# The attention's output projection, moved from the tail into the last chunk of the attention

## The chip, the cores and the metric

The kernel runs on one core of one Trainium2 chip. The metric is the device time of one launch in microseconds (us). Before the change the median of three runs is 10759.1 us (10754.76 to 10764.04). About 0.2% can be told from no change.

## What is computed

A four-layer graph network on N = 3327 nodes with 128 features and a dense 0/1 adjacency matrix. Only layer 1, an attention, and the start of layer 2 matter here.

```
def _L1_gnn_ref(x, spatial_encoding, edge_encoding, Wq, Wk, Wv, Wo):
    n, d = x.shape
    h = Wq.shape[0] // d
    scale = d ** (-0.5)
    q = (x @ Wq.T).reshape(d, n, h)
    k = (x @ Wk.T).reshape(d, n, h)
    v = (x @ Wv.T).reshape(d, n, h)
    a = jnp.einsum('dnh,dmh->dnm', q, k) * scale
    a = a + spatial_encoding + edge_encoding
    a = jax.nn.softmax(a, axis=2)
    out = jnp.einsum('dnm,dmh->dnh', a, v)
    out = out.reshape(n, h * d)
    return out @ Wo.T
...
    # --- layer 1 (adj_preln) ---
    h = jnp.maximum(_layernorm(x, axis=-1), 0.0)
    x = x + _L1_gnn_ref(h, adj, adj, L1_gnn_Wq, L1_gnn_Wk, L1_gnn_Wv, L1_gnn_Wo)
    # --- layer 2 (adj_preln) ---
    h = jnp.maximum(_layernorm(x, axis=-1), 0.0)
    x = x + _L2_gnn_ref(h, adj, ...)
```

There are 128 heads (d) of 8 features (h). The reshape is a plain one: the result in the order head, node, feature is cut into 3327 rows of 1024. So row r of what meets Wo holds the 128 pairs of head and node from 128 r on, and four heads in a row fill 4 x 3327 / 128, about 104 rows. A row is complete once the heads that it holds are done for all of its nodes.

## The kernel before, in words

**Order.** Layer 0, then the projections to queries, keys and values (written to device memory as qf, kf, vd), then the attention, then `tail`, which holds the output projection and layers 2 and 3. All but the tail stand in a manual schedule: each engine executes its instructions in the order in which the program emits them. In the tail the framework orders the instructions by itself, and what depends on nothing in the attention may be put far ahead (the load and scaling of the degrees, L1202 to L1204, runs in the attention's last chunk).

**The attention.** The queries are cut into seven chunks of 476 columns (the last has 471, handled as 472). In each chunk the 128 heads go by in 32 groups of four. In a group, the 26 tiles of 128 keys are worked off in blocks: in the first chunk pairs, later eight blocks of three tiles and one of two. For a block of three tiles:

- PE makes the scores of 12 (tile, head) pairs, in products of one to three heads (L926). Nine go to DVE, which adds the doubled adjacency tile and writes `p_early` (L942; sums of two heads or one, 944 or 472 elements). Three go to `late`.
- ACT takes the exponential of `late` (L956, 1416 elements) and of `p_early` (L947, 4248 elements).
- POOL multiplies the late ones by exp of the adjacency (L958).
- PE weighs: it multiplies by the values, with a column of ones for the sums of the softmax, into `acc` (L969). It weighs about eight tiles behind the products.

Within a block the order is a string, such as "aWAWbWBlc" and, every other block, "cWaWAbWlB"; the block of two has "WcWalA" or "WaWAlc". Letters a, A, b, B and c are products and sums, W weighs a tile, l is the late part. The score banks are two pairs in PSUM, taken in turn (`banks.pair()`), so PE runs at most two products ahead of DVE's sums. `late` has one buffer, p_early four.

**Between blocks** `events(c, g, t, ...)` is called for each tile t of the block just emitted. At t = 4 it loads the next group's keys (SP). At t = 8 it loads the next group's queries and values: a POOL memset of one column (L649), eight query loads (L654) and four value loads (L639), all issued by SP. When the last tile of a group has been weighed, in the third block of the next group, DVE copies `acc` out (L980) and SP stores it to `ot` in device memory with four DMAs (L985). `ot` has nine rows, eight features and the sum.

**The tail** first loads x (`xs_late`, L1092), which waits for the last store of the 16-bit adjacency (L887), and then projects: for 26 tiles of rows, a load of `o` from `ot` (L1185), the reciprocal of the sums (L1187, DVE), the division (L1188, DVE), eight transposes (L1193, PE), two copies of the transposed tile (L1194, ACT), eight products with Wo (L1197, PE, two instructions each), and the addition to x (L1198, DVE). `done` starts a piece of the layernorm (L162 to L169) and the split into two 16-bit parts (L219, L223) whenever its tiles are there: pieces of 4, 9 and 13 tiles. Then comes layer 2's aggregation over the adjacency, 14 products per tile (L235), and, after each second tile, four transposes of h (L1223).

Of the kernel before, what the change touches and what calls it, by code (L numbers as in the profile page):

```python
# [20 lines left out]
P = 128  # L21
N = 3327
# [34 lines left out]
def kernel(  # L57
# [83 lines left out]
    def in_pieces(f, cuts=CUTS):  # L141

        todo = [slice(t0, t1) for t0, t1 in zip(cuts, cuts[1:]) if t1 > t0]

        def done(t):
            while todo and todo[0].stop <= t:
                p = todo.pop(0)
                f(p, p.stop - p.start)

        return done  # L150

    def layernorm_relu(pool, then=None, tmp=None):

        h = pool.tile([P, T, D], F32, name="h")
        xc = (tmp or pool).tile([P, T, D], F32, name="ln_xc")
        sq = (tmp or pool).tile([P, T, D], F32, name="ln_sq")
        mean = pool.tile([P, T], F32, name="ln_mean")
        var = pool.tile([P, T], F32, name="ln_var")
        rstd = pool.tile([P, T], F32, name="ln_rstd")

        def piece(p, n):
            nc.vector.tensor_reduce(mean[:, p], xs[:, p], AX.X, ALU.add)  # L162
            nc.vector.tensor_scalar_mul(mean[:, p], mean[:, p], 1.0 / D)
            nc.vector.tensor_sub(xc[:, p], xs[:, p], over_t(mean, p.start, n))
            nc.scalar.activation(sq[:, p], xc[:, p], AF.Square)
            nc.vector.tensor_reduce(var[:, p], sq[:, p], AX.X, ALU.add)
            nc.scalar.activation(rstd[:, p], var[:, p], AF.Sqrt, bias=eps_c, scale=1.0 / D)
            nc.vector.reciprocal(rstd[:, p], rstd[:, p])
            nc.vector.scalar_tensor_tensor(h[:, p], xc[:, p], 0.0, over_t(rstd, p.start, n), op0=ALU.max, op1=ALU.mult)  # L169
            if then is not None:  # L170
                then(h, p, n)

        return h, in_pieces(piece)

    def load_rows(dst, src, t, col0, w):

# [92 lines left out]
    vd = dpool.tile([GP, EA], F32, name="vd")  # L269
    ot = dpool.tile([EA, GP], F32, name="ot")  # L270
    adj16 = dpool.tile([T, P, N], BF16, name="adj16")
    keyd = dpool.tile([NH // 4, P, NP], F16, name="keyd")

    q_chunks = chunks(N, QW)
# [241 lines left out]
    for n, t in enumerate(order):  # L516
        kp = rows_of(t)
        if t in kept:
            part_products(acc, n, parts1, t, kept[t], range(len(CS)), False)
            src = kept[t][:kp, : q_chunks[0][1]]  # L520
        else:
            a = early_a.pop(0) if early_a else load_a(t)
            part_products(acc, n, parts1, t, words(a)[:, :, 1], range(len(CS)), False)
            src = a[:kp, : q_chunks[0][1]]
        firsts[t] = doubled(adj_pools[0], src, t, q_chunks[0][1])
        add_to_sum(firsts[t], 0, n == 0)
        if n == 0:
            nc.vector.tensor_reduce(x_max, x1.rearrange("p t d -> p (t d)"), AX.X, ALU.max, apply_absolute_value=True)
        if n == 1:
            bit_limits()  # L530
            nc.gpsimd.dma_start(vd[N * NH : N * NH + 1, :], zero[:1, :EA])
            for end in (qf, kf):
                nc.gpsimd.dma_start(end[:E, N * NH :], zero[:E])
    for t in TAIL:
# [41 lines left out]
    class Parting:  # L576
# [7 lines left out]

        def load(self, side):
            src = SIDES[side][0]
            self.raw[side] = kq0.tile([E * JW, WJ], F32, name="raw")
            nc.sync.dma_start(self.raw[side], self.rows(src, 0))

        def part(self, side, i):  # L590
            if i == 0:
                self.hi[side] = kq0.tile([E * JW, WJ], F16, name="hi")
                self.lo[side] = kq0.tile([E * JW, WJ], F16, name="lo")
            p = slice(i * W4, min((i + 1) * W4, WJ))
            raw, hi = self.raw[side][:, p], self.hi[side][:, p]
            nc.gpsimd.tensor_copy(hi, raw)
            nc.gpsimd.tensor_sub(self.lo[side][:, p], raw, hi)  # L597
# [6 lines left out]
        def at(self, t):  # L604

            for side, t0 in ((0, 6), (1, 16)):
                if t0 <= t < t0 + 4:
                    self.part(side, t - t0)
                if t == t0 + 4:
                    self.store(side)  # L610
            if t == 10:
                self.load(1)

    PARTING_TILES = (6, 7, 8, 9, 16, 17, 18, 19)

# [176 lines left out]
    for r in range(T):  # L792
# [27 lines left out]
                early.pop(0)()  # L820
        if r % 2 and r // 2 < len(CS):
            store_x(r // 2)
        if r == 1:
            dp = ps.tile([P, 512], F32, name="tp")
            end = sum_columns(0, dp)
            sums = l1.tile([P, 512], F32, name="deg_sums", bufs=1)
            for n, c0, c1 in ((SUM_ROWS, QW, end - 1), (QW % SUM_ROWS, end - 1, end)):
                nc.vector.tensor_copy(sums[:n, c0:c1], dp[:n, c0:c1])
            store_sums(0, sums)
            nc.sync.dma_start(degd[:, N:], zero[:1, :1])  # L830
# [41 lines left out]
    with tc.tile_pool(name="at_in", bufs=1) as a_pool, tc.tile_pool(name="at_p", bufs=4) as p_pool, tc.tile_pool(  # L872
# [114 lines left out]
        with tc.manual_schedule(engines=engines), ExitStack() as ctx_ps:  # L987
# [19 lines left out]
                n_weighed += 1  # L1007

            def events(c, g, t, n, a_in):
                nonlocal coming, part, ahead_part, n_stored, k_next  # L1010
                more = n < len(groups)
                if t == 8 and more:
                    coming = first[n] if n < len(first) else load_rest(*groups[n])
# [19 lines left out]
                if t == 6 and c + 1 < len(q_chunks):  # L1033
                    for _ in range(min(len(to_store), 1 + T // n_groups)):
                        store_adj(*to_store.pop(0))
                    a_in += [load_adj(c + 1, i) for i in range(len(a_next), T * (g + 1) // n_groups)]
                if t == T - 4 and c + 1 < len(q_chunks):
                    for a, i, w in a_in:
                        a_next.append(doubled(adj_pools[(c + 1) % 2], a[: rows_of(i), :w], i, w))
                        to_sum.append((a_next[-1], c + 1, i == 0))  # L1040
                        to_store.append((c + 1, i, a_next[-1]))

            coming = part = None
            for n, (c, g) in enumerate(groups, 1):
                if n > 1:
                    q4, v4 = coming
# [8 lines left out]
                for i, size in enumerate(TRIPLES if c else PAIRS):  # L1055
# [9 lines left out]
                    for step in order:  # L1065
                        if step == "W":
                            if n_tiles + heads / 2 >= n_weighed + ahead:
                                weigh_next()
                        elif step == "l":
                            block.late_ones()  # L1070
                        else:
                            pos, which = PIECES[step] if step != "c" else (size - 1, (3,))
                            heads += len(which)
                            block.sums(pos, which, c > 0)
                    n_tiles += size
                    n_block += 1
                    for t in range(t0, t0 + size):
# [4 lines left out]
                            e_next.append(exp_of(a_next[late_tiles[len(e_next)]], c + 1))  # L1082
            while to_weigh:
                weigh_next()
            for a in to_store:
                store_adj(*a)

# [67 lines left out]
    def tail(general):  # L1155
# [13 lines left out]
        with ExitStack() as s:  # L1169
# [3 lines left out]
            def halved(h, p, n):  # L1173
                split_unless_general(parts, h, p, scale=PART)

            h, done = layernorm_relu(pool, halved)
            with tc.tile_pool(name="lo", bufs=3) as lo, tc.tile_pool(name="lo_ps", bufs=2, space=PSUM) as ps:
                wo_s = lo.tile([NH, E, D], F32, name="wo_s", bufs=1)
                nc.gpsimd.dma_start(wo_s, wo)
                for t in range(T):  # L1180
                    kp = rows_of(t)
                    o = lo.tile([P, EA, NH], F32, name="o")
                    src = ot.rearrange("e (p t c) -> t p e c", t=T, c=NH)[t]
                    for p0, p1 in ((0, kp),) if kp == P else ((0, 112), (112, kp)):
                        nc.sync.dma_start(o[p0:p1], src[p0:p1])  # L1185
                    inv = lo.tile([P, NH], F32, name="inv")
                    nc.vector.reciprocal(inv[:kp], o[:kp, E, :])  # L1187
                    nc.vector.tensor_mul(o[:kp, :E, :], o[:kp, :E, :], inv[:kp].unsqueeze(1).to_broadcast([kp, E, NH]))  # L1188
                    oT = lo.tile([NH, E, P], F32, name="oT")
                    for quad in range(2):  # L1190
                        tp = ps.tile([P, 4, P], F32, name="tp")
                        for j in range(4):
                            nc.tensor.transpose(tp[:, j, :kp], o[:kp, 4 * quad + j, :], ident[:kp, :kp])  # L1193
                        nc.scalar.copy(oT[:, 4 * quad : 4 * quad + 4, :kp], tp[:, :, :kp])  # L1194
                    yp = ps.tile([P, D], F32, name="yp")
                    for e in range(E):
                        nc.tensor.matmul(yp[:kp], oT[:, e, :kp], wo_s[:, e, :], start=(e == 0), stop=(e == E - 1))  # L1197
                    nc.vector.tensor_add(xs[:kp, t, :], xs[:kp, t, :], yp[:kp])  # L1198
                    done(t + 1)

            if not general:
                nc.sync.dma_start(deg, degd.rearrange("o (p t) -> (o p) t", t=T))  # L1202
# [404 lines left out]
```

## Time and profile before

| what | us |
|---|---|
| median of three runs | 10759.1 |
| the profiled execution's own time | 10759.11 |
| its span, first to last instruction | 10757.4 |
| DVE, ACT, PE, POOL busy in the span | 10089.7, 9935.9, 9785.6, 7294.7 |
| L942 DVE, sums of the scores | 9151.8 |
| L947 and L956 ACT, exponentials | 8123.9 and 3908.6 |
| L958 POOL, products of the late part | 6397.6 |
| last L969 ends, first L235 starts | 10036.35, 10145.50 |

Busy times are of the hardware profiler; an instruction can start in its engine's pipeline before the one ahead of it has left, so the sum over a line can exceed its share of the span. A wait is written as idle time before an instruction, with what ended it. The profile also gives the TensorE clock that was granted, as a share of full speed: 0.988 on average.

### The profile page before, as it was taken

What the parts mean: (1) busy time and instruction counts of PE and PEld (TensorE: products, weight loads), DVE (VectorE), ACT (ScalarE), POOL (GpSimd) and SP (SyncE); (2) the same over time, 40 slices, a digit from 0 to 9 for tenths busy, and PEclk for the clock granted to TensorE, in tenths of its full rate; (3) what the DMA queues carried; (4) which work ended last, traced back from release to release, by engine and by line L of the source; (5) the groups of instructions that cost most, each with busy time, mean ns of one, the idle gap of its engine ahead of it and who ended that gap; (6) DMA issues with size and microseconds to landing.
All of it is one profiled execution on the core that took longest, in us unless ns stands there. A gap on an engine that the chain in (4) does not pass through costs nothing. (4 is left out here: it accounts for less than half of the span.)

```text
span 10757.4 us, 183790 instructions
## 1 busy us (share of the span) xinstructions
PE 9785.6 (91%) x74235; PEld 2140.8 (20%) x74268; DVE 10089.7 (94%) x11602; ACT 9935.9 (92%) x4716; POOL 7294.7 (68%) x3314
## 2 busy tenths in 40 slices
PE   7899999999989999899999999999999989999897
PEld 3211111111111111111111111111111111111453
DVE  5799999999999999999999999999999999999666
ACT  2799999999999999999999999999999999999432
POOL 3388887777777777777777777777777766666203
PEclk9999999999999999999999999999999999999998
DMA  8644433111111111111111111111111111111422
GB/s 294 205 105 104 103 99 87 45 42 45 45 42 45 44 44 43 45 45 43 46 44 44 42 45 46 42 45 43 43 42 44 46 36 38 35 37 38 160 92 101
DMA packets 462641, 709.21 MB, mean 66 GB/s; under 512 B 56587, under 2 KB 391419, under 8 KB 456150
## 3 DMA queue, kind: packets, MB, share of 16 engines
q1 hardware_dynamic: 458596, 690.86, 21.7%
q8 instruction: 585, 9.58, 0.4%
q0 software_dynamic: 3184, 6.51, 0.2%
q14 instruction: 276, 2.26, 0.1%
HBM read 557.43 MB, written 139.73 MB: 65 GB/s over the span
## 5 line engine op out<-in xcount | busy, mean ns | idle before, releaser
L942 DVE TENSOR_TENSOR p_early<-early,a 128x952 f32<-128x952 f32 (+3 forms) x10336 | 9151.8, 957 | 172.3 <-PE early L926 141.3
L947 ACT ACTIVATE p_early<-p_early 128x4284 f32<-128x4284 f32 (+3 forms) x2144 | 8123.9, 3789 | 8.9 <-DVE p_early L942 8.5
L958 POOL TENSOR_TENSOR p_late<-p_late,e 128x1428 f32<-128x1428 f32 (+3 forms) x2144 | 6397.6, 2984 | 2521.4 <-ACT p_late L956 2505.8
L969 PE MATMUL acc<-p_early,v 128*9 128x476 f32 (+3 forms) x33728 | 5704.9, 565 | 126.7 <-issue 114.4
L956 ACT ACTIVATE p_late<-late 128x1428 f32<-128x1428 f32 (+1 forms) x2144 | 3908.6, 1823 | 12.4 <-DMA vd<-v_st 5.3
L926 PE MATMUL early<-q,k_in 32*128 32x476 f16 (+1 forms) x14784 | 3058.5, 366 | 440.1 <-DVE p_early L942 417.3
L969 PE MATMUL acc<-p_late,v 128*9 128x476 f32 (+3 forms) x12864 | 2101.0, 565 | 0.2 <-POOL p_late L958 0.2
L926 PEld LDWEIGHTS <-k_in 32*128 32x128 f16 x19968 | 764.9, 91 | 5446.0 <-issue 5425.1
L926 PE MATMUL late<-q,k_in 32*128 32x476 f16 (+1 forms) x5184 | 778.5, 367 | 178.8 <-ACT p_late L956 178.6
L969 PEld LDWEIGHTS acc<-p_early,v 128*9 128x9 f32 (+1 forms) x33728 | 655.6, 88 | 1197.1 <-issue 1038.7
L926 PE MATMUL early<-q,k 32*128 32x476 f16 x2080 | 395.6, 368 | 6.9 <-DVE p_early L942 5.2
L969 PEld LDWEIGHTS acc<-p_late,v 128*9 128x9 f32 (+1 forms) x12864 | 240.5, 88 | 458.4 <-issue 363.0
L235 PE MATMUL agg_ps<-a,part 128*128 128x512 bf16 (+1 forms) x1067 | 240.8, 378 | 53.1 <-issue 47.4
L926 PEld LDWEIGHTS <-k 32*128 32x128 f16 x3328 | 121.3, 91 | 786.5 <-issue 770.5
L194 ACT ACTIVATE agg<-agg_ps 128x512 f32<-128x512 f32 x9 | 4.7, 598 | 256.6 <-PE agg_ps L235 256.6
L358 PE MATMUL agg_ps<-a,part 128*128 128x512 bf16 (+4 forms) x720 | 171.1, 395 | 56.6 <-DMA a<-in_adjT_dram 55.3
L666 DVE TENSOR_REDUCE k<-k_in 128x256 f16<-128x256 f16 x377 | 221.8, 588 | 0.0
L285 POOL TENSOR_SCALAR a<-a_in 128x476 bf16<-128x476 f32 (+2 forms) x156 | 219.0, 1404 | 0.5
L597 POOL TENSOR_TENSOR lo<-raw,hi 96x278 f16<-96x278 f32 (+1 forms) x256 | 182.3, 712 | 20.5
L296 POOL TENSOR_TENSOR deg_half<-deg_half,a 128x476 f32<-128x476 f32 (+1 forms) x175 | 191.9, 1096 | 2.1
L955 PE MATMUL late<-a,two_i 128*128 128x476 bf16 x544 | 182.2, 373 | 0.0
L1386 PE MATMUL sp<-yT,hT 128*128 128x512 f32 (+1 forms) x364 | 171.3, 612 | 11.6 <-ACT agg L1391 5.7
(289 smaller groups left out, 2693.2 us busy)
## 6 DMA issues: line engine op xcount, KB each, us to landing
k_in<-keyd SPq DMA_DIRECT2D x192, 832.0 KB
v<-vd SPq DMA_DIRECT2D x896, 117.0 KB
a<-in_adjT_dram SPq DMA_DIRECT2D x39, 1663.5 KB
a<-adj SPq DMA_DIRECT2D x78, 831.8 KB
a_in<-in_adjT_dram SPq DMA_DIRECT2D x125, 238.0 KB
keyd<-k SPq DMA_DIRECT2D x416, 64.0 KB
k_in<-kt SPq DMA_DIRECT2D x240, 104.0 KB
q<-qt SPq DMA_DIRECT2D x1520, 14.9 KB
```

Source lines behind the costliest of these rows:

```text
L235: nc.tensor.matmul(acc[c][:, :w], part[:, t, :], a[:, c0 : c0 + w], start=(t == 0 and i == 0), stop=(t == T - 1 and i == len(parts) - 1),)
L285: nc.gpsimd.tensor_scalar(a2[:kp, :w], a, 2.0 * S_SCALE, None, op0=ALU.mult)
L296: nc.gpsimd.tensor_tensor(deg_half[:, :w], deg_half[:, :w], a2[:, :w], op=ALU.add)
L597: nc.gpsimd.tensor_sub(self.lo[side][:, p], raw, hi)
L666: nc.vector.tensor_reduce(k, src.unsqueeze(3), AX.X, ALU.max)
L926: return nc.tensor.matmul(sp[:, : self.we], self.keys(self.t0 + pos)[r], self.q4[r, : self.we], start=True, stop=stop)
L942: Block.first_sum = nc.vector.tensor_tensor(p, scores, a2, op=ALU.add)
L947: nc.scalar.activation(p, p, AF.Exp, scale=1.0 / S_SCALE)
L955: nc.tensor.matmul(late[:, i, :we], two_i, self.a[pos][:, :we], start=False, stop=True)
L956: nc.scalar.activation(self.late[:, :, :we], late[:, :, :we], AF.Exp, scale=1.0 / S_SCALE)
L958: nc.gpsimd.tensor_tensor(g, g, self.e[:, :we].unsqueeze(1).to_broadcast([P, self.n_g, we]), op=ALU.mult)
L969: nc.tensor.matmul(acc[32 * i : 32 * i + EA, :w], self.v4[:kp, i, t, :], p[:kp, :w], start=(t == 0), stop=(t == T - 1),)
```

## The change

Four edits belong together.

1. A class `Rows` works off the rows of one head group: `load` fetches them from `ot` (about 104 rows of 9 x 128, two DMAs), `invert` and `divide` make the softmax's division, `turn` transposes the eight features, and `project` multiplies by Wo and stores about 104 rows of the product to a new scratch `yo` (two DMAs).
2. In the last chunk, group g does this for group g - 1: load at event t = 11, reciprocal on DVE at t = 14, division on POOL in two halves at t = 17 and t = 20, the transposes in the eighth block behind its step "A", with the copy on DVE, and the projection in the ninth block behind its step "A". Both take a pair of score banks. Wo is loaded by SP in the first group, into the buffers that the first chunk's key pairs used. The last group's rows follow after the last weighing, with the division on DVE, and ahead of the last store of the adjacency.
3. The tail loads `yo` in three DMAs (the last five partitions hold what the last group wrote), adds it to x in five pieces of 2, 4, 6, 7 and 7 tiles, and starts the layernorm in the same pieces. The old projection stays for a general case that isn't run here.
4. To make room, the buffers `raw`, `hi` and `lo` of the first chunk get a shape that `Rows` can share, hi and lo as halves of one tile. The degree sums of the first chunk move from row tile 1 to row tile 12 of the layer's projections. A row of zeros is written to the end of `yo`.

```
+    yo = dpool.tile([NP, D], F32, name="yo")
...
+            nc.gpsimd.dma_start(yo[N:], zero[:1, :D])
...
-            self.raw[side] = kq0.tile([E * JW, WJ], F32, name="raw")
+            self.raw[side] = kq0.tile([P, EA * NH], F32, name="raw")[: E * JW, :WJ]
...
-                self.hi[side] = kq0.tile([E * JW, WJ], F16, name="hi")
-                self.lo[side] = kq0.tile([E * JW, WJ], F16, name="lo")
+                parts = kq0.tile([P, 2, WJ + 1], F16, name="parts")
+                self.hi[side], self.lo[side] = (parts[: E * JW, j, :WJ] for j in range(2))
...
+    class Rows:
+        def __init__(self, g):
+            self.r0 = 4 * g * N // NH
+            self.m = 4 * (g + 1) * N // NH - self.r0
+            self.pieces = ((0, 96), (96, self.m))
+        def load(self):
+            self.o = kq0.tile([P, EA * NH], F32, name="raw").rearrange("r (e c) -> r e c", c=NH)
...
+            for p0, p1 in self.pieces:
+                nc.sync.dma_start(self.o[p0:p1], src[self.r0 + p0 : self.r0 + p1])
+        def invert(self):
+            nc.vector.reciprocal(self.inv, self.o[: self.m, E, :])
+        def divide(self, engine, e0, n):
+            o = self.o[: self.m, e0 : e0 + n]
+            engine.tensor_tensor(o, o, self.inv.unsqueeze(1).to_broadcast([self.m, n, NH]), op=ALU.mult)
+        def turn(self, tp):
+            m = self.m
+            for e in range(E):
+                nc.tensor.transpose(tp[:, e // 4, e % 4 * m : (e % 4 + 1) * m], self.o[:m, e, :], ident[:m, :m])
+            nc.vector.tensor_copy(self.oT.rearrange("c (a r) -> c a r", a=2), tp[:, :, : 4 * m])
+        def project(self, yp, wo_s):
+            m = self.m
+            for e in range(E):
+                nc.tensor.matmul(yp[:m, 0, :D], self.oT[:, e * m : (e + 1) * m], wo_s[e], start=(e == 0), stop=(e == E - 1))
+            nc.vector.tensor_copy(self.y, yp[:m, 0, :D])
+            for p0, p1 in self.pieces:
+                nc.sync.dma_start(yo[self.r0 + p0 : self.r0 + p1], self.y[p0:p1])
...
-        if r == 1:
+        if r == 12:
...
+                if c + 1 == len(q_chunks) and g == 0 and t == 2:
+                    for e in range(E):
+                        k = kq0.tile([P, 2, P], F16, name="k", bufs=KEYS_AHEAD + 1)
+                        wo_s.append(k.bitcast(F32).rearrange("p a b -> p (a b)"))
+                        nc.sync.dma_start(wo_s[e], wo[:, e, :])
+                if c + 1 == len(q_chunks) and g:
+                    if t == 11:
+                        rows = Rows(g - 1)
+                        rows.load()
+                    if t == 14:
+                        rows.invert()
+                    if t in (17, 20):
+                        rows.divide(nc.gpsimd, 0 if t == 17 else 4, 4)
...
+                        if step == "A" and rows and i == 7:
+                            rows.turn(banks.pair()[0])
+                        if step == "A" and rows and i == 8:
+                            rows.project(banks.pair()[0], wo_s)
+                            rows = None
...
+            rows = Rows(n_groups - 1)
+            rows.load()
+            rows.invert()
+            rows.divide(nc.vector, 0, E)
+            rows.turn(banks.pair()[0])
+            rows.project(banks.pair()[0], wo_s)
             for a in to_store:
                 store_adj(*a)
...
+            h, done = layernorm_relu(pool, halved, cuts=CUTS if general else X_CUTS)
+            if not general:
+                y = pool.tile([P, T, D], F32, name="y")
+                by_slot = yo.rearrange("(p t) d -> p t d", t=T)
+                last = 4 * (NH // 4 - 1) * N // NH // T
+                for p0, p1 in ((0, 112), (112, last), (last, P)):
+                    nc.sync.dma_start(y[p0:p1], by_slot[p0:p1])
+                for t0, t1 in zip(X_CUTS, X_CUTS[1:]):
+                    nc.vector.tensor_add(xs[:, t0:t1], xs[:, t0:t1], y[:, t0:t1])
+                    done(t1)
```

More of the change, by code (lines that the diff above doesn't have):

```diff
@@ L150, in in_pieces, with layernorm_relu @@
         return done
-    def layernorm_relu(pool, then=None, tmp=None):
+    def layernorm_relu(pool, then=None, tmp=None, cuts=CUTS):
         h = pool.tile([P, T, D], F32, name="h")
@@ L171, in piece @@
                 then(h, p, n)
-        return h, in_pieces(piece)
+        return h, in_pieces(piece, cuts)
     def load_rows(dst, src, t, col0, w):
@@ L612, in at @@
                 self.load(1)
+    class Rows:
[5 more added lines that the diff above has]
+            self.o = kq0.tile([P, EA * NH], F32, name="raw").rearrange("r (e c) -> r e c", c=NH)
+            rest = kq0.tile([P, 2, WJ + 1], F16, name="parts").bitcast(F32).rearrange("p a b -> p (a b)")
+            m = self.m
+            self.oT, self.y, self.inv = rest[:, : E * m], rest[:m, E * m : E * m + D], rest[:m, E * m + D : E * m + D + NH]
+            src = ot.rearrange("e (r c) -> r e c", c=NH)
+            for p0, p1 in self.pieces:
[11 more added lines that the diff above has]
+        def project(self, yp, wo_s):
+            m = self.m
+            for e in range(E):
[3 more added lines that the diff above has]
+                nc.sync.dma_start(yo[self.r0 + p0 : self.r0 + p1], self.y[p0:p1])
     PARTING_TILES = (6, 7, 8, 9, 16, 17, 18, 19)
@@ L1009, in events @@
             def events(c, g, t, n, a_in):
-                nonlocal coming, part, ahead_part, n_stored, k_next
+                nonlocal coming, part, ahead_part, n_stored, k_next, rows
                 more = n < len(groups)
@@ L1041, in events @@
                         to_store.append((c + 1, i, a_next[-1]))
-            coming = part = None
+            coming = part = rows = None
+            wo_s = []
             for n, (c, g) in enumerate(groups, 1):
@@ L1174, in halved @@
                 split_unless_general(parts, h, p, scale=PART)
[L1176 to L1199, printed above, removed]
@@ new lines, in tail @@
+            h, done = layernorm_relu(pool, halved, cuts=CUTS if general else X_CUTS)
[8 more added lines that the diff above has]
+                    done(t1)
+            else:
+                with tc.tile_pool(name="lo", bufs=3) as lo, tc.tile_pool(name="lo_ps", bufs=2, space=PSUM) as ps:
+                    wo_s = lo.tile([NH, E, D], F32, name="wo_s", bufs=1)
+                    nc.gpsimd.dma_start(wo_s, wo)
+                    for t in range(T):
+                        kp = rows_of(t)
+                        o = lo.tile([P, EA, NH], F32, name="o")
+                        src = ot.rearrange("e (p t c) -> t p e c", t=T, c=NH)[t]
+                        for p0, p1 in ((0, kp),) if kp == P else ((0, 112), (112, kp)):
+                            nc.sync.dma_start(o[p0:p1], src[p0:p1])
+                        inv = lo.tile([P, NH], F32, name="inv")
+                        nc.vector.reciprocal(inv[:kp], o[:kp, E, :])
+                        nc.vector.tensor_mul(o[:kp, :E, :], o[:kp, :E, :], inv[:kp].unsqueeze(1).to_broadcast([kp, E, NH]))
+                        oT = lo.tile([NH, E, P], F32, name="oT")
+                        for quad in range(2):
+                            tp = ps.tile([P, 4, P], F32, name="tp")
+                            for j in range(4):
+                                nc.tensor.transpose(tp[:, j, :kp], o[:kp, 4 * quad + j, :], ident[:kp, :kp])
+                            nc.scalar.copy(oT[:, 4 * quad : 4 * quad + 4, :kp], tp[:, :, :kp])
+                        yp = ps.tile([P, D], F32, name="yp")
+                        for e in range(E):
+                            nc.tensor.matmul(yp[:kp], oT[:, e, :kp], wo_s[:, e, :], start=(e == 0), stop=(e == E - 1))
+                        nc.vector.tensor_add(xs[:kp, t, :], xs[:kp, t, :], yp[:kp])
+                        done(t + 1)
```

## The prediction

> **What bounds the kernel now.** I read the sums by stretch first, for the last chunk of the attention (about 8700 to 10036 us) and for the stretch behind it, because the change lives in these two. The columns are PE, PEld, DVE, ACT and POOL busy, then the granted PE clock and the DMA share.
>
> ```profile
> 9400.00:9800.00 400.00, 364.80 (x2953) 67.11 (x2951) 393.46 (x418) 400.00 (x171) 275.35 (x96) 1.00 0.12 36
> 10045.00:10141.00 96.00, 82.02 (x617) 75.29 (x616) 69.06 (x97) 33.14 (x60) 4.70 (x11) 0.92 0.57 172
> ```
>
> ACT is busy for 400.00 of 400.00 us: the exponentials bound the last chunk, and any us in which ACT stands still is lost. DVE idles 6.54 us of 400, which is 0.7 us in a head group. A group takes 42.28 us (the stores of its result start at 9913.92, 9956.57 and 9998.48). The second stretch is the projection in the tail, where ACT is nearly idle.
>
> Second view, the timeline of one group in the last chunk, engine by engine. The store to ot at 9744.80 belongs to the group before, and this group's next queries and values are fetched on SP behind it.
>
> ```profile
> 9744.14 0.64 DVE L980 COPY o<-acc 105x471 f32<-105x471 f32 x1
> 9744.69 27.75 DVE L942 TENSOR_TENSOR p_early<-early,a 128x944 f32<-128x944 f32 x29
> ...
> 9752.33 0.12 POOL L649 MEMSET q<- 128x1 f16 x1
> ...
> 9768.67 3.23 POOL L958 TENSOR_TENSOR p_late<-p_late,e 128x1416 f32<-128x1416 f32 x1 [1.66 <-ACT p_late L956]
> ...
> 9752.47 5.06 SPq L654 DMA_DIRECT2D q<-qt  x8
> 9757.63 1.78 SPq L639 DMA_DIRECT2D v<-vd  x4
> ```
>
> The reader is to see the order of SP: the eight query loads can't leave before POOL's memset at 9752.33, which stands behind POOL's multiplication of the third block, and with the value loads they hold SP to 9759.41. In DVE, 29 sums take 27.75 us, so a block of five takes 4.78 us. ACT's period is 4.87 us (the late exponentials start at 9747.07 and 9751.94). DVE runs ahead of ACT by little.
>
> Third view, the waits around 8735 us. There the kernel already has, once, what the change will do in every group: a DVE instruction between the sums that waits for a load (the degrees).
>
> ```profile
> 8734.89 0.91 DVE L1203 TENSOR_SCALAR deg<-deg 128x26 f32<-128x26 f32 x1 [4.59 <-DMA deg<-degd]
> 8735.71 3.29 DVE L942 TENSOR_TENSOR p_early<-early,a 128x944 f32<-128x944 f32 x4
> ...
> 8737.49 3.74 ACT L947 ACTIVATE p_early<-p_early 128x4248 f32<-128x4248 f32 x1 [4.97 <-DVE p_early L942]
> 8741.97 1.35 ACT L956 ACTIVATE p_late<-late 128x1416 f32<-128x1416 f32 x1 [0.74 <-PE early L926]
> 8743.52 3.75 ACT L947 ACTIVATE p_early<-p_early 128x4248 f32<-128x4248 f32 x1 [0.20 <-DVE p_early L942]
> ```
>
> DVE waited 4.59 us and worked 0.91 us, and ACT stood still for 4.97 + 0.74 + 0.20 = 5.9 us. The stores of ot around it are 8724.84 and 8773.31, 48.47 us apart instead of 42.28. **Price: a DVE wait of 4.6 us costs the kernel 6.2 us**, 1.6 us more than the wait.
>
> **What the change removes.** In the tail, PE ends the attention at 10036.35 and starts the next aggregation (L235) at 10145.50: 109 us. Between lie 26 tiles of load, reciprocal, product, transposes and projection:
>
> ```profile
> L1197 PE MATMUL yp<-wo_s,oT 128*128 128x128 f32 (+1 forms) x416 | 58.1, 296 | 7.8 <-ACT oT L1194 7.8
> L1188 DVE TENSOR_TENSOR o<-o,inv 128x1024 f32<-128x1024 f32 (+1 forms) x26 | 31.7, 1221 | 0.6
> L1187 DVE RECIPROCAL inv<-o 128x128 f32<-128x128 f32 (+1 forms) x26 | 24.5, 946 | 13.3 <-DMA o<-ot 13.2
> ```
>
> **What stays there.** The last group's rows, in a chain: copy of acc 0.65 and four stores to 10038.6; landing 2 us; load 4.3 us (the first o load went out at 10036.51, and its reader started at 10040.80), so 10044.9; reciprocal 0.95 and product 1.22, 10047.1; eight transposes on a cold PE 1.94 (the first eight at 10043.12), 10049.0; copy 0.95, 10050; 16 matmuls 2.05 to 4.09, 10053; copy 0.28 and two stores, 10054. Behind them in SP's order stands the last store of adj16, and the load of x waits for it, as it did before (3.9 us); both landings take about 2.8 us (the degree load, 8732.13 to 8734.89), so x leaves near 10057. x and y are 1.66 MB each; at the 340 GB/s that the DMA sum shows while o is loaded they need 10 us and 2 us to land: 10069. One addition (0.28) and the layernorm of two tiles, ten short instructions of 0.15 to 0.4 us (a thirteen-tile pass is 1.89) with their hand-overs, 4 to 5 us: PE starts at about 10075. **Gain 70 us**; 85 if the loads of x and y overlap the chain, 55 if weights and a16 tiles get in the way. The other pieces keep ahead of PE: DVE needs about 0.8 us a tile (six passes of 1.89/13), PE 3.0 us.
>
> **What each of 31 groups pays.** A group's rows now go through the in-order queues of ACT's feeders.
>
> 1. The load (event 11, after the fourth block) stands on SP behind the queries and values: it leaves at 9759.5 and, with the 4.3 us of the first o load (576 KB, here 468), lands at 9763.8. The reciprocal (event 14) stands on DVE right after the fifth block. DVE is there at 9744.69 + 2.9 (three sums) + 2 x 4.78 = 9757.1. It waits 6.5 us, and queued behind it are the sums of the sixth block, for which PE's banks, and then ACT, wait. With the price above: 6.5 + 1.6 = 8.1 us. Its own 0.95 stands for the degrees' 0.91.
> 2. The second half of the division (event 20) stands on POOL behind the product of the seventh block, which ends at 9768.67 + 3.23 = 9771.9. Its 512 elements take 512/1416 of 3.23 = 1.2 us, so 9773.1. PE comes to the transposes after the second product of the eighth block, before DVE ends that sum at 9757.1 + 2 x 4.78 + 2.1 = 9768.8. PE waits there with all products behind, and DVE waits in its copy of oT: to 9773.1 plus four transposes (0.5) and a hand-over, 4.9 us. Today ACT starts a block's late exponentials when DVE ends that block (9766.53 against 9766.7); after a stall they go as soon as PE's late product is out, about a sum (1.05) earlier against DVE, and POOL with them. So 3.7 to 4.9; I take 4.2, which costs 5.8.
> 3. The projection, 16 matmuls of 2.05 us in a row in PE, holds the products of the next block, with 0.3 us of copy on DVE. Between 0 (PE idles 9% of 42 us) and 2.3, as no row shows it: I take 1.0, because ACT has about 5 us of work in hand there.
>
> Sum 14.9 us, for 30 groups 447; the last group fetches no queries and values, so its first wait goes: 7. **Together 454 us.** Bounds for one group: 11 if a stall costs hardly more than its wait, 18.5 if every stall starts without lead and 2 us of slow clock follow.
>
> A rule to weigh. The degrees' stall left PE idle for 5.08 us, and the granted clock then stood at 0.51 from 8735.3 to 8742.2; that loss is inside my price. The Trainium skill, "TensorE: Matmul & The Clock Gate", Part 1, warns of gaps over some 3.4 us and prices each at one window of 3.4 us at half clock, and its example throttles 5.2 us after the last matmul. The row throttles after 3.5 us and stays low for two windows. If each of the two stalls paid the page's 1.7 us on top of its delay, rather than the 0.7 that is left of my 1.6 when the 0.91 of work is taken off, the sum would be 62 us more.
>
> **Costed at nothing.** The eight wo loads on SP, 0.4 us each, go out once in a queue that has nothing due. The zeros for yo, one descriptor-sized transfer on POOL, stand beside two like them. hi and lo in one tile: each side's parts were already split after the other side's store. The degree sums of the first chunk move from row tile 1 to 12: ten matmuls of 0.22 us that nobody waits for at 260 us; if they collide there, 2 us either way. The two yo stores follow DVE's copy on SP with nothing due before the next keys.
>
> **Sum.** +454 - 70 = +384 us. The profiled execution took 10759.11 us with a span of 10757.4, which is the median of the runs (10759.1), so 11143, rounded to **11140 us**.
>
> **Rivals.**
> - Faster: the rows arrive in time, and only work counts. DVE gets 0.95 + 0.95 + 0.28 = 2.2 us more in a group and has 0.7 free, so 1.5 x 31 = 46 lost against 70: 10735. The point that decides is SP: the rows would have to be in SBUF when DVE ends the fifth block, 6.5 us earlier than the queue allows, and POOL's half would have to end before PE's eighth block. For it: the emission leaves a block (4.9 us) between the steps. Against it: SP's and POOL's rows above. Nine in 100, two of them near no change.
> - One stall alone: if DVE falls behind so far at the first that POOL is done when PE arrives, (8.1 + 1.5) x 31 - 70 = +228, 10985; if the load is early and the second stays, (5.8 + 1.5) x 31 - 70 = +156, 10915. Fourteen in 100.
> - Worse: the stalls leave no lead and PE is cold after both, 18.5 x 31 - 55 = +520, 11280 and more. Ten in 100.
> - It doesn't do what it says, and the tail keeps its length behind y: +454 - 20, 11190; it lies inside the range.
>
> **How the numbers follow.** Both stalls, near 15 us a group: 67 in 100, from 11015 (11 x 31 - 85) to 11260. The range reaches down to 10950, to take in half of the one-stall cases, and up to 11280. About 0.2% (22 us) is what can be told from no change. Faster 7, same 2, slower 91 in 100.
>
> **What would show it.** Right: the starts of the ot stores in the last chunk 55 to 60 us apart; DVE waiting some 6 us for the o load before each reciprocal, PE some 4 us for POOL before the transposes; ACT no longer at 100%; granted clock below 1.0 through slices 33 to 37; PE's first L235 some 35 to 40 us after the last L969. Wrong: ACT still at 100% there, the o load landing before the fifth block ends, or a tail that is not shorter.

## The result, and the profile after

The changed kernel takes 11186.33 us (median of four runs, 11182.33 to 11191.43) against 10758.48 us before: ratio 1.0397, 95% interval 1.0379 to 1.0416. It is slower by 428 us, forecast were 381. The profiled execution has a span of 11186.5 us, 429.1 more than before's.

The sums by stretch, for a stretch of the last chunk (in each line the busy time of PE, PEld, DVE, ACT and POOL, then the granted PE clock, the DMA share and GB/s):

```profile
9400.00:9800.00 400.00, 313.81 (x2326) 68.56 (x2324) 306.71 (x326) 300.04 (x125) 218.62 (x84) 0.88 0.13 37
```

ACT, which was busy for 400 of 400 us, is now busy for 300. The granted clock, 1.00 before, is 0.88. A head group takes 57.7 us on average instead of 42.28 (DVE's copies of acc run from 8687.80 to 10476.10 us, 31 groups apart).

One group in the timeline, DVE first, then POOL, PE and SP. Its first wait is the longest of 24, which average 5.7 us; the mean follows below:

```profile
9972.51 0.95 DVE L634 RECIPROCAL parts<-raw 104x128 f32<-104x128 f32 x1 [6.60 <-DMA raw<-ot]
...
9990.06 1.02 DVE L644 COPY parts<-early 128x832 f32<-128x832 f32 x1 [3.23 <-PE early L643]
...
10000.09 0.29 DVE L650 COPY parts<-early 104x128 f32<-104x128 f32 x1 [1.41 <-PE early L649]
...
9984.58 3.21 POOL L998 TENSOR_TENSOR p_late<-p_late,e 128x1416 f32<-128x1416 f32 x1 [0.74 <-ACT p_late L996]
9987.75 1.26 POOL L638 TENSOR_TENSOR raw<-raw,parts 104x512 f32<-104x512 f32 x1
...
9989.06 0.96 PE L643 MATMUL early<-ident,raw 104*128 104x104 f32 x4 [2.64 <-POOL raw L638]
...
9959.68 5.06 SPq L694 DMA_DIRECT2D q<-qt  x8
9964.85 2.89 SPq L679 DMA_DIRECT2D v<-vd  x4
9967.78 0.92 SPq L631 DMA_DIRECT2D raw<-ot  x2
```

The reader is to see three waits of DVE. The rows' load goes out at 9967.78, right behind the queries and values, and DVE's reciprocal starts on the rows 4.7 us later; by then DVE has stood for 6.60 us. Four transposes wait on PE for POOL's second half, which ended at 9989.01, and DVE waits for them in its copy. A block later DVE waits 1.41 us for the projection. ACT's own waits in this group, the number in brackets, follow them:

```profile
9977.95 1.35 ACT L996 ACTIVATE p_late<-late 128x1416 f32<-128x1416 f32 x1 [7.95 <-PE early L966]
...
9992.83 1.35 ACT L996 ACTIVATE p_late<-late 128x1416 f32<-128x1416 f32 x1 [4.69 <-PE early L966]
...
10000.47 1.35 ACT L996 ACTIVATE p_late<-late 128x1416 f32<-128x1416 f32 x1 [2.33 <-PE early L966]
10004.74 1.35 ACT L996 ACTIVATE p_late<-late 128x1416 f32<-128x1416 f32 x1 [0.85 <-PE early L966]
```

In sum over 24 groups (9000 to 10400 us), the waits of DVE:

```profile
DVE parts L634 <- DMA raw<-ot: 137.9, 24, 6.6
...
DVE p_early L982 <- PE early L966: 91.7, 123, 1.2
DVE parts L644 <- PE early L643: 75.6, 25, 3.7
...
DVE parts L650 <- PE early L649: 24.6, 24, 1.5
```

That is 5.7 us a group for the load, 3.0 for the transposes, 1.0 for the projection, and 3.8 for score products that come late. In the kernel before, only the last of these stands in the list (8800 to 9800 us), with 0.6 a group:

```profile
DVE p_early L942 <- PE early L926: 13.4, 35, 0.5
```

The tail did get shorter: the last weighing ends at 10522.63, the aggregation starts at 10573.52, 50.9 us instead of 109.2. What follows takes 613.0 us, 611.9 before.

### The profile page after: what moved, and what is told of

Same layout as the page of the kernel before. It is cut to its first block, busy times and chain, and to the rows that moved or that the text cites. A ratio compares the mean times of both kernels' runs of the same rounds, so it can differ in the third digit from the quotient of the medians.

```text
span 11186.5 us, 184194 instructions
## 1 busy us (share of the span) xinstructions
PE 9922.5 (89%) x74379; PEld 2155.7 (19%) x74412; DVE 10122.4 (90%) x11640; ACT 9941.1 (89%) x4670; POOL 7375.3 (66%) x3376
## 5 line engine op out<-in xcount | busy, mean ns | idle before, releaser
L987 ACT ACTIVATE p_early<-p_early 128x4284 f32<-128x4284 f32 (+3 forms) x2144 | 8024.9, 3743 | 34.8 <-DVE p_early L982 33.3
L1009 PE MATMUL acc<-p_early,v 128*9 128x476 f32 (+3 forms) x33728 | 5796.3, 575 | 125.6 <-issue 113.6
L996 ACT ACTIVATE p_late<-late 128x1428 f32<-128x1428 f32 (+1 forms) x2144 | 3811.8, 1778 | 432.5 <-PE early L966 399.1
L599 POOL TENSOR_TENSOR parts<-raw,parts 96x278 f16<-96x278 f32 (+1 forms) x256 | 182.8, 714 | 20.5
L634 DVE RECIPROCAL parts<-raw 104x128 f32<-104x128 f32 (+1 forms) x32 | 30.5, 953 | 178.6 <-DMA raw<-ot 178.6
```

What stands on the lines that cost most here:

```text
L987: nc.scalar.activation(p, p, AF.Exp, scale=1.0 / S_SCALE)
L996: nc.scalar.activation(self.late[:, :, :we], late[:, :, :we], AF.Exp, scale=1.0 / S_SCALE)
L1009: nc.tensor.matmul(acc[32 * i : 32 * i + EA, :w], self.v4[:kp, i, t, :], p[:kp, :w], start=(t == 0), stop=(t == T - 1),)
```

## The experiments

Changes are shown against the changed kernel, or against the experiment that is named. Times are medians of 2 to 10 runs. The kernel before ran beside each of three sets of experiments, with 10753.8, 10756.5 and 10757.0 us. So a difference between two sets carries some 3 us.

**The first wait: SP's order.** The load is put ahead of the queries and values, nothing else.

```
+                if t == 8 and c + 1 == len(q_chunks) and g:
+                    rows = Rows(g - 1)
+                    rows.load()
                 if t == 8 and more:
                     coming = ...
...
-                    if t == 11:
-                        rows = Rows(g - 1)
-                        rows.load()
```

> The changed kernel with the rows' load put at event 8, ahead of the loads of the next queries and values on SP; nothing else is moved. Theory one, the two waits (SP's order makes DVE wait at the reciprocal, POOL's order makes PE wait at the transposes): the first wait, 5.8 us a group in the mean, goes, and 1 to 2 us of slow clock and lost lead with it; 30 groups make 200 to 230 us, so 10955 to 10985, with a group of about 51 us instead of 58. Theory two, the added work and the score banks it takes are what costs, and a wait only shows where it lands: under 60 us less, above 11125, with the time turning up as a longer wait at the transposes.

Measured: 10964.19 us, 222 less. DVE's wait for the load is gone from the list (9000 to 9800 us), and a group takes 50.9 us. The wait at the transposes has hardly grown, 3.3 us each where it was 3.0:

```profile
DVE parts L644 <- PE early L643: 53.1, 16, 3.8
```

222 us over the 30 groups that fetch queries and values are 7.4 us, for a wait of 5.7 to 5.9. The first theory holds, and the second falls for this wait.

**The second wait: POOL's order.** The transposes go a block later, the projection into the next group (and, for the last of them, ahead of the remaining weighings).

```
-                        if step == "A" and rows and i == 7:
+                        if step == "A" and rows and i == 8:
                             rows.turn(banks.pair()[0])
-                        if step == "A" and rows and i == 8:
+                        if step == "A" and rows and i == 0:
                             rows.project(banks.pair()[0], wo_s)
```

> The changed kernel with the transposes put a block later (the ninth block) and the projection into the next group's first block; the load stays behind the queries and values. Theory one, the two waits: PE no longer waits for POOL's second half (3.0 us a group in DVE's row), and about 2 us of slow clock and lost lead go too, so 5 us in 31 groups, 11030 us; the first wait stays at about 6 us. Theory two, the added work: the transposes and the copy cost the same wherever they stand, within 40 us of 11186.

Measured: 11038.56 us, 148 less, 4.8 us a group. The wait at the transposes is gone from the list (9000 to 9800 us), and the wait for the load stays, 5.9 us each:

```profile
DVE parts L634 <- DMA raw<-ot: 87.9, 15, 6.4
```

**Both.** The load at event 8 as above, and POOL's halves right behind the reciprocal:

```
                     if t == 14:
                         rows.invert()
-                    if t in (17, 20):
-                        rows.divide(nc.gpsimd, 0 if t == 17 else 4, 4)
+                        rows.divide(nc.gpsimd, 0, 4)
+                        rows.divide(nc.gpsimd, 4, 4)
```

> Load at event 8 ahead of the queries and values, reciprocal at 14 as it was, and both halves of the division on POOL right at 14, two blocks ahead of the transposes. Theory one, the two waits: both go; what is left in a group is DVE's 2.3 us of work less its 0.7 us of slack and about 1 us behind the projection, 2.5 to 3.5 us, 80 to 110 in all, against the tail's 58 us and with the 8 us of the moved sums: 10790 to 10820, 0.3 to 0.6% over before, ACT at 93% or more in the last chunk and the clock at 1.0. Theory two, the added work and the banks: above 11000.

Measured: 10815.83 us, ratio 1.0054 (1.0038 to 1.0071). The same stretch:

```profile
9400.00:9800.00 400.00, 358.70 (x2931) 83.73 (x2931) 382.79 (x411) 374.95 (x157) 273.33 (x104) 1.00 0.17 46
```

ACT is back at 375 of 400 and the clock at 1.00. Against the version with the first wait alone taken away, this is again 148 us: by two different edits the second wait costs the same with and without the first, so these two add up. What is left in a group is 3.5 us.

**The moved degree sums.** A line that I had costed at nothing.

```
-        if r == 12:
+        if r == 1:
             dp = ps.tile([P, 512], F32, name="tp")
```

> The changed kernel with one edit undone: the degree sums of the first chunk go back from row tile 12 to row tile 1. The trace of the changed kernel stands 7.6 us behind before's when the attention's first group ends, and loses them between 350 and 364 us, beside the stores of the sums. Theory one, the moved stores cost them: 7 to 8 us less than the changed kernel, about 11179 us, and the first copy of acc at 485 us as before. Theory two, the load phase scatters by that much from run to run: no difference beyond the spread of 10 us, and the copy still at 492 us.

Measured: 11175.41 us, 11 less than the changed kernel, but the first copy of acc came at 477 us, not at 485: the loads of layer 0 scatter by several us, so this run doesn't decide by its total. The same edit on the version with both waits away:

> The version with both waits taken away, with the degree sums back at row tile 1. Theory one (the moved stores of the sums cost 7 to 8 us of the projections): 10808 us. Theory two (the load phase only scatters): 10816, no difference.

Measured: 10806.72 us, 9 less; taken from the kernel before beside each, 6 less. And the moved sums in the kernel before, which is otherwise unchanged:

> The kernel before with the degree sums at row tile 12 instead of 1, and nothing else. Theory one: their 476 stores of four bytes stand in the way of the projections' stores, which ACT waits for: 7 to 10 us slower, 10762 to 10765, with one wait of ACT for the stores of about 8 to 11 us near 360 us where before has 4. Theory two: the load phase scatters, no difference.

Measured: 10766.56 us, 10 more; its ratio of 1.0007 has an interval of 0.9998 to 1.0017, so the total alone is short of telling. The wait of ACT for the projections' stores tells. First the kernel before, then the sums moved alone, then the sums moved back:

```profile
356.83 1.02 ACT L688 ACTIVATE qk_st<-pp 128x1024 f32<-128x1024 f32 x1 [3.98 <-DMA qf<-qk_st]
```
```profile
367.41 1.02 ACT L688 ACTIVATE qk_st<-pp 128x1024 f32<-128x1024 f32 x1 [10.16 <-DMA qf<-qk_st]
```
```profile
352.24 1.02 ACT L728 ACTIVATE qk_st<-pp 128x1024 f32<-128x1024 f32 x1 [3.87 <-DMA qf<-qk_st]
```

In the changed kernel it is 11.07 us. Three pairs of totals give 6 to 11 us, none of them clear by itself. The traces decide: in all five with the sums at row 12 the longest of these waits is 7.7 to 11.1 us and the first store of the attention's result goes out at 487 to 497 us; in all nine with the sums at row 1 it is 3.5 to 4.7 us, and the store goes out at 478 to 486. The first theory holds. At row 1 (259 to 265 us) no such wait follows the stores; at row 12 (343 to 352 us) the same stores stand on SP ahead of the stores that ACT waits for. That the number of four-byte pieces is what holds these back, and not another part of the moved sums, is read from the wait and was not tried apart.

**What is left: DVE's work?** From the version with both waits away and the sums back, the reciprocal goes to POOL (`minus` is a column of -1):

```
-                        rows.invert()
+                        nc.gpsimd.tensor_tensor(rows.inv, rows.o[: rows.m, E, :], minus[: rows.m].to_broadcast([rows.m, NH]), op=ALU.pow)
```

> As the one before, with the reciprocal of the sums taken from DVE and made on POOL, as a power of -1, ahead of the two halves of the division. If what is left in a group (3.5 us) is DVE's work, 0.95 us of it goes in 31 groups: 30 us less than that version, 10780. If it is the projection on PE and the score banks, nothing goes. The price of the power on POOL is unknown; POOL has 9 us free in a group, and above that it would come late for the transposes, and slower than the version before.

Measured: 11341.84 us, ratio 1.0547. It doesn't answer the question, because the power takes POOL 20.7 us a group, and the transposes wait for POOL. (POOL had more room than the 9 us expected: it is busy for 274 of 400 us in the version before, so some 14 us of a group of 46 are free. The power overran that too.)

```profile
L1089 POOL TENSOR_TENSOR parts<-raw,minus 104x128 f32<-104x128 f32 x13 | 269.5, 20727 | 0.0
```

**The copy behind the projection.** On top of an earlier store of the adjacency (next experiment), DVE's copy of y is emitted behind the next sum.

```
                             block.sums(pos, which, c > 0)
+                            if done_rows:
+                                done_rows.pop(0).keep()
```

> As the one before, with DVE's copy of the projected rows put behind the next sum instead of right behind the matmuls. DVE waits 1.0 us a group for PE there. If that wait is lost time, 20 to 30 us less than the kernel before it, 10765 to 10775, within 0.2% of the kernel before the change. If PE's 16 matmuls hold back the next products anyway, and with the bank held for longer, no gain or a few us worse.

Measured: 10811.54 us against 10802.69: no gain. The wait moved from the copy (16.9 us in 17 groups, now none) to the sums (37.3 us for PE, 11.2 with the copy where it was).

**PE, DVE and the tail apart.** Three kernels that leave work out, with yo filled by a copy of x. First the tail alone: the events of the rows are taken out of the chunk for 31 groups.

> The tail's half of the change alone: no rows are loaded, inverted, divided, turned or projected in the last chunk for the first 31 groups (one copy of x fills yo instead, so x is added in place of the projection); the last group's rows and the tail are as in the version with both waits away and the sums back. If the tail's gain is what it was in the changed kernel (50.9 us from the last weighing to the aggregation instead of 109.1), 10697 us; the rest of the way to 10807 is then the price of the rows in the chunk.

Measured: 10694.36 us, ratio 0.9943 (0.9926 to 0.9959): the tail's half is worth 62.6 us against the kernel before beside it (10756.95), and the sum of the rows in the chunk, with both waits away, is 10806.7 - 10694.4 = 112 us, 3.6 a group (116 if each is taken from the kernel before beside it).

Then everything but the projection:

```
                         if step == "A" and rows and i == 8:
-                            rows.project(banks.pair()[0], wo_s)
                             rows = None
```

> The version with both waits away and the sums back, without the 16 matmuls of the projection, DVE's copy behind them and the two stores, in the first 31 groups (yo is filled with a copy of x). If the burst on PE and the wait behind it cost most of the 3.5 us that are left in a group, about 2 us a group go: 10745. If DVE's work is the cause, only the 0.28 us of the copy goes: 10795.

Measured: 10749.38 us, so the projection costs 57 us, 1.85 a group (61 us if each is taken from the kernel before beside it), and the rest 55. The rest points to DVE's added work: in this version DVE is as full as in the kernel before, with 394 of 400 us, though a group is 1.8 us longer, and ACT is not:

```profile
9600.00:10000.00 400.00, 358.58 (x2916) 70.77 (x2908) 394.47 (x419) 389.68 (x165) 286.12 (x109) 1.00 0.17 48
```

And PE's part alone, without any copy, reciprocal or division:

```
+            if alone:
+                return
             nc.vector.tensor_copy(self.oT.rearrange("c (a r) -> c a r", a=2), tp[:, :, : 4 * m])
...
-                nc.tensor.matmul(yp[:m, 0, :D], self.oT[:, e * m : (e + 1) * m], wo_s[e], start=(e == 0), stop=(e == E - 1))
+                lhs = wo_s[e][:, :m] if alone else self.oT[:, e * m : (e + 1) * m]
+                nc.tensor.matmul(yp[:m, 0, :D], lhs, wo_s[e], start=(e == 0), stop=(e == E - 1))
+            if alone:
+                return
             nc.vector.tensor_copy(self.y, yp[:m, 0, :D])
```

> The same version with PE's part of the rows alone in the first 31 groups: the load, the eight transposes and the 16 matmuls stay (with Wo in the place of the rows), while the reciprocal, POOL's division, both DVE copies and the stores are left out. PE has about 3.7 us free in a group and gets 2.8 us more. If DVE's work and waits are what is left, under 0.5 us a group: 10697 to 10715. If PE's work fills the group by itself, 2 to 3 us a group: 10760 to 10790.

Measured: 10776.64 us, 82 more than the tail alone, 2.65 a group. The theory that only DVE's work and waits are left, which had this under 0.5 us a group, falls. PE's 2.9 us cost nearly all of themselves, though PE idles 9% of the chunk. It isn't all: 30 of the 112 us come only with DVE's and POOL's part. DVE's waits for products in 800 us show what PE's part does, first with the tail alone, then with PE's part added:

```profile
DVE p_early L981 <- PE early L965: 10.5, 28, 0.5
```
```profile
DVE p_early L986 <- PE early L970: 51.8, 72, 1.4
```

In the second, 2.9 us in each of 18 groups. PE idles as long in a group as without the bursts, 3.9 us for 3.7: the added work used none of that time. With the tail alone, PE's idle time lies in pieces of 0.4 us on average and 1.0 at most, spread over the group; the two bursts last 0.9 and 2.0 us. That they don't fit into such pieces, and that PE's lead over DVE, two pairs of banks, of which each burst holds one, doesn't bridge them, is the reading that fits. Bursts cut into smaller pieces, or with banks of their own, were not run.

**The head of the tail.** The last store of the adjacency, for which the loads of x and of the weights wait, is put ahead of the last group's rows. The head of the tail is the time from the last weighing to the aggregation.

```
             while to_weigh:
                 weigh_next()
+            for a in to_store:
+                store_adj(*a)
             rows = Rows(n_groups - 1)
```

> The version with both waits away and the sums back, with the last store of the adjacency ahead of the last group's rows instead of behind them. The loads of x and of the tail's weights wait for this store. If the tail's head is set by these loads (the weights' biases reach DVE 18 us after they are issued), 12 to 18 us go: about 10793. If it is set by the last group's rows and y, under 4 us go.

Measured: 10802.69 us, 4 less than without, which is within the spread of the runs, and the head of the tail is not shorter (49.8 us against 48.4; versions with the same tail show 48.4 to 50.9). The loads did go earlier, but the sum of two biases in DVE's queue, which the framework places, now stands ahead of the reciprocal and waits for them:

```profile
10162.47 0.16 DVE L1169 TENSOR_TENSOR b_rz<-b_ih_s,b_hh_s 128x3 f32<-128x3 f32 x1 [19.12 <-DMA b_hh_s<-in_b_hh_dram]
```

So the test was spoilt by a new wait; how much of the 50 us lies in the loads stays open. No version beat the kernel before: the best with all of the work is 0.4% slower (1.0043, 1.0029 to 1.0057).

## Why the prediction was right, and where its sizes were off

The difference splits into parts, each a difference of two medians: 10694 (tail alone, sums back) + 112 (rows without waits) + 9 (sums) + 148 (second wait) + 222 (first wait) = 11185, against 11186 measured. The sum closes by construction, as each run is the next one's start; the only test in it is that the second wait gives 148 with the first wait there and without it.

| step of the prediction | forecast, us | measured, us |
|---|---|---|
| the tail gets shorter | -70 | -63 |
| first wait: load behind queries and values | 243 (8.1 x 30) | 222 (7.4 x 30) |
| second wait: transposes behind POOL | 180 (5.8 x 31) | 148 (4.8 x 31) |
| what else the rows cost | 31 (1.0 x 31) | 112 (3.6 x 31) |
| degree sums moved | 0, 2 either way | 6 to 11 |

The rows of the table don't hold the same work. The forecast's two waits contain 0.9 us of DVE's work each; the measured ones don't, as the reciprocal and the copy stay in the experiments. With that work put to the rest, the forecast is 367 us for the waits and 87 for the rest, against 370 and 112.

- **The mechanism was right.** Both waits stand where the order of SP and of POOL put them, and each goes when its order is changed. The rival "faster" fails at the point that it named, SP: the load goes out behind the queries' and values' issues, when DVE's reciprocal is already waiting for it.
- **That 367 met 370 is luck.** The waits are shorter than worked out (5.7 us for 6.5, 3.0 for 4.2), and each costs more above its length: 1.5 to 1.8 us (7.4 for 5.7 to 5.9, 4.8 for 3.0 to 3.3), where the forecast, without the work, had 0.7. That price was also read a little high. The groups of the kernel before alternate between 41.9 and 42.65 us; against the longer kind, to which it belongs, the degrees' stall cost 5.8 us and not 6.2, and the next group was 0.5 us shorter than its kind. So one stall at the chunk's start was no good measure of a stall in every group.
- **"I take 1.0" for the projection was the term that was too small.** Its reason, that ACT has 5 us in hand, was wrong: the projection alone costs 1.85 us a group. The transposes with DVE's copy and reciprocal cost 1.8 more, for which the forecast had 0.9 twice.
- **The costing of the degree sums at nothing failed.** It named the row at 260 us, where nobody waits, and not the place they move to. Ten matmuls are cheap; their 476 stores of four bytes on SP, which the prediction didn't count, stand in the way of others there.
- **The tail**: 58.3 us less in the changed kernel's own trace, for 70, so the sign "35 to 40 us after the last weighing" failed with 50.9. Counted from there, yo's last stores leave at 20.4 us (17.7 forecast), because the load of the last rows goes out 3.5 us after the last store to ot and not 2, and its reader starts 5.7 us later and not 4.3; the load of x leaves at 22.9 (20.7 forecast). The addition of x and y, forecast for 33, starts at 43.7. Ahead of it in DVE's queue stands the sum of the two biases, which waits for the weights, whose loads start only behind the last store. The kernel before has this wait too (6.17 us at 10054.26), and the prediction didn't name it:

```profile
10565.22 0.16 DVE L1169 TENSOR_TENSOR b_rz<-b_ih_s,b_hh_s 128x3 f32<-128x3 f32 x1 [8.68 <-DMA b_hh_s<-in_b_hh_dram]
```

- **The miss.** Counted like this, the miss of some 45 us lies in one direction: 25 too little for the rows' work, 10 for the sums, 7 too much gain, and 3 for the waits.
- **The clock.** Only the first wait left: 0.92 to 0.93 in the stretch; only the second: 0.95; neither: 1.00. In the group shown above, the clock fell to 0.50 at 9988.5, 2.1 us into PE's wait for POOL and 2.9 us behind the last score product, and stood there for 10 us. The Trainium skill, "TensorE: Matmul & The Clock Gate", Part 1, lets the clock drop after an idle window of about 3.4 us. The runs agree in direction, and show a drop with less. What the clock costs by itself was not tried apart, so how much of the 1.5 to 1.8 us above a wait is clock, and how much lost lead, stays open.

## What to carry to other kernels

Before work is put into the slack of a pipeline, read for each of its instructions what stands ahead of it in its own queue, and when that leaves: a load was late by the twelve loads ahead of it, a division by the product ahead of it, and the program's distance of a block said nothing about either. Slack counts in the pieces in which it comes: here an engine that idled 9% of the time, in pieces of at most 1 us, had no room for bursts of 0.9 and 2.0 us. And an edit that only moves something is priced at the place it goes to, with its transfers.

## What the runs showed that I had not expected

- Eight transposes and 16 small matmuls, 2.9 us of PE's time, cost 2.65 us a group on a PE with 3.7 us of idle time in it.
- A power of -1 over 104 x 128 elements takes POOL 20.7 us; the reciprocal takes DVE 0.95.
- With stores of 476 single floats put into a busy phase of stores, the longest wait for the next ones grows by 4 to 7 us.
- The two stalls of this pipeline add: the second wait cost 148 us with the first one there and without it.
